# Weights' loads behind the preceding product, and the projection's loads a step later, in a two-block image kernel

## The chip, the cores and the metric

The kernel runs on one core of a Trainium2 chip. A core has a matrix engine (TensorE, PE in the profile; its weight loads are shown as PEld), a vector engine (VectorE, DVE), an activation engine (ScalarE, ACT), a general engine (GpSimd, POOL) and an engine that mostly issues transfers (SyncE, SP). The engines run side by side, each works through its own list of instructions in order, and they wait for each other through semaphores. Transfers between the chip's large memory and the on-chip memory are issued from SP, ACT and POOL.

The metric is the time of one launch on the device in microseconds (us), the median of several runs. Everything is float32.

## The reference, cut to what matters

32 images of 96 x 56 x 56 go through two blocks, and then one normalisation over the whole batch.

```python
# block 0, per image: expand, depthwise 3x3, gate by channel, project, add
h = silu(bn1(conv1x1(x, w1)))            # 96 -> 576 channels
h = silu(bn2(depthwise3x3(h, w2)))
s = sigmoid(W2 @ silu(W1 @ mean_hw(h)))  # one number a channel
x = x + bn3(conv1x1(h * s, w3))          # 576 -> 96: "the projection"

# block 1, per image
mag  = abs(rfft2(x));  ca = gate by channel from mag
sa   = gate by pixel from mean, norm and spectrum of x
y    = x * ca * sa
freq = resize(mean_c(abs(rfft2(y))))
aux  = concat([y, coord, freq])
off  = conv3x3(aux)                      # 9 taps x (dx, dy) a pixel
gate = sigmoid(conv1x1(relu(conv3x3(aux))))
base = conv3x3(y)
smp  = bilinear samples of y at pixel + tap + off
z    = (1 - gate) * base + gate * (def_w . smp)
# at the end, over all images: out = relu(batchnorm(z) + x)
```

## The kernel before, in words

The main part is one long program, `layers`. It works on three images at a time. For image b the main loop samples and convolves block 1, band by band: 7 bands of 8 rows, and each band in two halves. Beside it run two generators: `second(b + 1)` (the function `attend`), which does the gate, the projection, the two Fourier stages and the attention of the next image, and `first(b + 2)` (`hidden`), which expands and does the depthwise convolution of the image after that. `pump` calls them step by step: a band has 17 slots (7 steps of each half, and three more), and each slot lets each generator go on until it has done its share of its steps. `second` has 61 steps, spread over 108 slots of the image's 119. A `yield` in a generator is the end of a step, so an additional `yield` is an empty step.

**The weights.** Sampling is a matrix product. For each half band, weights of 128 x 1008 are made as the product of two tiles, `wc` and `wr`, on VectorE (`weights`, line 692: `wc = wc * wr`). Each of the two tiles is loaded in two parts of 252 KB from `hd` in the large memory, so that is four loads a half band (`weights_load`, lines 685 and 686), issued by SP. There are 448 such products (32 images x 14). `hd` of a band comes from a chain: the offsets are copied out by VectorE (line 651), POOL writes them to memory as `od` (line 655), SP loads them spread over partitions as `ht` (line 667), ScalarE makes hats of them (lines 670 and 671) and writes `hd` (line 674).

`prepare(upto)` issues loads until `upto` products have theirs, and not beyond the bands whose `hd` is written. With `AHEAD = READY = 1`, half band k = 2n + h calls `prepare(k + 2)` at its start, which issues the loads of product k + 1; product k + 1 itself stands in the same half band, behind the first of the two sampling groups (`ready.extend(weights(...))`). `wc` has 3 buffers and `wr` has 2: the loads of product m wait until the sampling of half band m - 3 has read its `wc` (line 721) and until product m - 2 is done.

**The projection.** An image of block 0's hidden values (`h2d`, in the large memory) is read back in 4 pairs of row groups. Each pair has two loads, `hq0` (4 units, 784 KB) and `hq1` (5 units, 980 KB), by `project_loads` (line 305), each with a single buffer. `project` multiplies `hq0` in one step (8 matrix instructions of line 323), then `hq1` in a later step (8 more of line 323 and 4 of line 329). The results go through ScalarE (line 333), POOL adds the residual (line 466) and stores them to `x1d` (line 467). After the fourth pair the first Fourier stage (`dft_mag`) loads `x1d` back (line 361) and multiplies it (lines 386 and 410); its squares are summed on VectorE (line 414).

**Who sets the order.** A scheduler orders the instructions of PE, DVE, ACT and POOL; the order in which the code writes them is its priority. SP is excepted: `tc.manual_schedule(engines={SP})` keeps its instructions in the order of the code. SP therefore holds everything back that stands behind a load that has to wait.

The lines that the change touches are 450 to 468 of `attend` and 1114 to 1135 of the main loop.

## Time and profile before

| | us |
|---|---|
| median of 3 runs (9661.39 to 9698.82) | 9661.97 |
| the profiled execution, own time | 9648.5 |
| its span, first to last instruction | 9646.7 |
| PE busy | 8472.7 (88%) |
| DVE busy | 7227.2 (75%) |
| ACT busy | 5322.1 (55%) |
| POOL busy | 2532.6 (26%) |
| 16 DMA engines' time, the SP queue (q1) | 37.9% of the span |

The page gives, for each engine, the time in which it worked. "Waits" lists name an instruction by engine, tile and line, what it waited for, the total of such waits, how many there were and the longest. The timeline gives the start, the duration, the engine, the line, the operation and the tiles, and in brackets the engine's idle time just before and what ended it. The profile also records the clock that TensorE was granted: in this execution it is either full or half, 0.923 in the mean.

### The profile page before, as it was taken

The page shows a single profiled execution, that of the slowest core. Times are in us where ns is not written, and L with a number is a line of the kernel's source. Part 1 is how long each engine was busy: PE and PEld are TensorE (multiplying, and loading weights), DVE is VectorE, ACT ScalarE, POOL GpSimd, SP SyncE. Part 2 cuts the span into 40 slices and gives each one's busy share as a digit, 9 for nine tenths or more (in the row PEclk, how much of TensorE's full clock was granted, in tenths as well). Part 3 has the DMA queues.
Part 4 walks back from the last instruction along what each step waited for, and adds up shares of the span by engine and source line. Part 5 has one row for each costly group of instructions (what it writes and reads, how often), then busy time and mean ns, then how long its engine had stood idle before and what let it go on. Part 6 is the DMA issues. An engine that isn't in the chain of part 4 may idle for free. (4 is left out here: it accounts for less than half of the span.)

```text
span 9646.7 us, 129705 instructions
## 1 busy us (share of the span) xinstructions
PE 8472.7 (88%) x48374; PEld 5064.2 (52%) x48374; DVE 7227.2 (75%) x6948; ACT 5322.1 (55%) x10262; POOL 2532.6 (26%) x2642
## 2 busy tenths in 40 slices
PE   6889989998999999999899989999999999999870
PEld 3455555555555555555555555555555555555540
DVE  7688777778777787877777887777878777777323
ACT  2355555565555556555555655555555555565453
POOL 1123223222222322222232322233222323322210
PEclk9899999999999999999999999999999999999985
DMA  2355555555555555555555555555555555554449
GB/s 94 95 143 148 151 152 160 150 149 143 147 155 154 160 154 145 145 149 155 154 160 155 145 142 153 151 158 154 153 139 145 150 157 157 153 152 135 130 154 417
DMA packets 1069473, 1485.98 MB, mean 154 GB/s; under 512 B 590438, under 2 KB 840086, under 8 KB 1056550
## 3 DMA queue, kind: packets, MB, share of 16 engines
q1 hardware_dynamic: 858747, 985.20, 37.9%
q10 hardware_dynamic: 153803, 329.80, 9.2%
q0 software_dynamic: 56288, 162.60, 6.7%
q8 instruction: 388, 6.36, 0.3%
q14 instruction: 247, 2.02, 0.1%
HBM read 1064.29 MB, written 412.65 MB: 153 GB/s over the span
## 5 line engine op out<-in xcount | busy, mean ns | idle before, releaser
L261 DVE SCALAR_TENSOR_TENSOR acch<-hp,w,acch 128x1512 f32<-128x1512 f32 (+1 forms) x2250 | 4320.5, 1920 | 32.8
L605 PE MATMUL mm<-yp,c_jointW 104*128 104x448 f32 x4032 | 1649.0, 561 | 9.0 <-ACT yt L709 5.5
L740 PE MATMUL pd<-v,c_def 128*96 128x224 f32 (+1 forms) x6272 | 1414.8, 376 | 127.6 <-ACT v L732 104.1
L703 POOL COPY ybl<-yp 96x448 f32<-96x448 f32 x896 | 1014.7, 1159 | 1903.7 <-PE mm L707 1903.3
L721 PE MATMUL mm<-wc,yt 64*96 64x144 f32 x12544 | 1168.1, 308 | 153.5 <-DVE yb L638 76.8
L740 PEld LDWEIGHTS pd<-v,c_def 128*96 128x96 f32 (+1 forms) x6272 | 1051.8, 173 | 437.4 <-ACT v L732 142.5
L168 PE MATMUL mm<-xt,w 96*128 96x392 f32 (+3 forms) x2688 | 1136.3, 561 | 133.8 <-ACT yt L709 96.0
L605 PEld LDWEIGHTS mm<-yp,c_jointW 104*128 104x128 f32 x4032 | 783.6, 196 | 806.0 <-issue 762.6
L721 PEld LDWEIGHTS mm<-wc,yt 64*96 64x96 f32 x12544 | 884.2, 167 | 489.8 <-issue 188.0
L221 ACT ACTIVATE acch<-acch,sh,inv 128x1568 f32<-128x1568 f32 x288 | 487.5, 1693 | 1159.0 <-DVE acch L261 1143.9
L692 DVE TENSOR_TENSOR wc<-wc,wr 128x1008 f32<-128x1008 f32 x448 | 564.6, 1260 | 704.2 <-DMA wr<-hd 690.5
L725 ACT COPY v<-mm 96x288 f32<-96x288 f32 (+1 forms) x2688 | 1003.6, 442 | 117.7 <-PE mm L721 78.9
L172 ACT ACTIVATE hp<-mm,sh,inv 128x392 f32<-128x392 f32 (+2 forms) x1216 | 811.8, 672 | 326.9 <-PE mm L168 282.1
L633 PE MATMUL mm<-yp,c_base0W 96*64 96x448 f32 x4032 | 913.5, 550 | 0.0
L323 PE MATMUL mm<-hq,w3s 128*96 128x392 f32 x2048 | 788.2, 531 | 127.4 <-DMA hq<-h2d 125.9
L655 POOL DMA_DIRECT2D od<-at x224 | 186.3, 832 | 2275.1 <-DVE at L651 1451.9
L732 ACT COPY v<-v 32x448 f32<-32x448 f32 x1344 | 755.3, 562 | 30.3
L168 PEld LDWEIGHTS mm<-xt,w 96*128 96x128 f32 (+1 forms) x2688 | 389.9, 189 | 495.1 <-issue 264.8
L709 ACT COPY yt<-mm 128x384 f32<-128x384 f32 (+1 forms) x896 | 350.9, 441 | 491.5 <-PE mm L707 489.4
L323 PEld LDWEIGHTS mm<-hq,w3s 128*96 128x96 f32 x2048 | 336.3, 173 | 477.7 <-issue 382.5
L466 POOL TENSOR_TENSOR o<-o,xc 96x392 f32<-96x392 f32 x256 | 396.5, 1549 | 643.9 <-ACT o L333 642.3
L633 PEld LDWEIGHTS mm<-yp,c_base0W 96*64 96x64 f32 x4032 | 294.6, 134 | 515.5 <-issue 490.2
(194 smaller groups left out, 9023.7 us busy)
## 6 DMA issues: line engine op xcount, KB each, us to landing
h2d<-acch ACTq DMA_DIRECT2D x288, 784.0 KB
wc<-hd SPq DMA_DIRECT2D x896, 252.0 KB
wr<-hd SPq DMA_DIRECT2D x896, 252.0 KB
hq<-h2d SPq DMA_DIRECT2D x128, 980.0 KB
hq<-h2d SPq DMA_DIRECT2D x128, 784.0 KB
x<-x1d SPq DMA_DIRECT2D x768, 98.0 KB
ht<-od SPq DMA_DIRECT2D x224, 252.0 KB
hd<-ht ACTq DMA_DIRECT2D x224, 252.0 KB
```

Source lines behind the costliest of these rows:

```text
L168: nc.tensor.matmul(pt[p0 : p0 + w1.shape[1], : rows * W], w1, xts[hf][:, r0 * W : (r0 + rows) * W], start=True, stop=True)
L172: nc.scalar.activation(h1[lo:hi, row0 : row0 + rows, 1 : 1 + W], pt[lo:hi, : rows * W].rearrange("p (h w) -> p h w", h=rows), AF.Silu, bia ...
L261: nc.vector.scalar_tensor_tensor(acc[:, lo:hi], win, wk, acc[:, lo:hi], ALU.mult, ALU.add)
L323: nc.tensor.matmul(pts[half][:C, :EW], w3s[:, ch], hq, start=(i == 0), stop=False)
L605: nc.tensor.matmul(view, weights[:, k], yp[:channels, r0 : r0 + RB, dx + PD - 1 : dx + PD - 1 + W], start=(k == 0), stop=(k == NTAP - 1))
L633: nc.tensor.matmul(pb[k % 2 * BC : (k % 2 + 1) * BC, :BW].rearrange("p (h w) -> p h w", h=RB), w["base"][:, k], yp[:C, r0 : r0 + RB, dx + ...
L692: nc.vector.tensor_tensor(wc, wc, wr, ALU.mult)
L703: nc.gpsimd.tensor_copy(yb[:, :, s], blocks)
L721: nc.tensor.matmul(pt[k][:C, (t - lo) * KP : (t - lo + 1) * KP], yt[ps, t], s[ps, t * KP : (t + 1) * KP], start=True, stop=True)
L725: nc.scalar.copy(v[:C, :, lo:hi, k].rearrange("c k t p -> c t k p"), pt[k][:C, : (hi - lo) * KP].rearrange("c (t k p) -> c t k p", t=hi - ...
L732: nc.scalar.copy(v[C:, 1 + 2 * i : 3 + 2 * i], v[i * QC : (i + 1) * QC, KA:])
L740: nc.tensor.matmul(out.rearrange("c q (t x) -> c t q x", x=TS), p["w"]["def"][ks, k], v[ks, k].rearrange("c t s (r x) -> c t (s r) x", r=T ...
```

## The change

```diff
 def attend(...):                       # the projection, pair q of 4
         for q in range(NQ):
+            if q:
+                yield
             at = q, q + NQ
             xrs = [residual_load(nc, p, x, k) for k in at]
             outs = project(nc, p, rows)
             next(outs)
             yield
+            yield
             if q + 1 < NQ:
                 first = project_loads(nc, p, h2d, q + 1, 0)
-            yield
             os = next(outs)
-            if q + 1 < NQ:
-                rows = [first, project_loads(nc, p, h2d, q + 1, 1)]
             yield
             for k, o, xr in zip(at, os, xrs):
                 nc.gpsimd.tensor_tensor(o, o, xr, ALU.add)
                 nc.gpsimd.dma_start(x1[:, k * EW : (k + 1) * EW], o)
+            if q + 1 < NQ:
+                rows = [first, project_loads(nc, p, h2d, q + 1, 1)]
             yield

 # the main loop, band n, half h
                 v = p["vp"].tile([128, NTAP, NTH, 2, TP], FP, name="v")
-                prepare(2 * n + h + READY + AHEAD)
                 s = ready.pop(0)
                 ...
                         ready.extend(weights(nc, *ws) for ws in loads[:1])
                         del loads[:1]
+                        prepare(2 * n + h + 1 + READY + AHEAD)
                         if h == 0:
                             yts.append(block_channels(nc, p, yp, j, 1))
```

Half band k now issues the loads of product k + 2, directly behind product k + 1, where before the loads of product k + 1 stood at the start of half band k. So each group of four loads stands four slots earlier in the code or, across a band's end, seven. In the projection, `hq0` of the next pair is issued two steps behind the product that frees its buffer (one step before), and `hq1` one step behind its own (in the same step before). Pairs 1 to 3 have 5 steps instead of 4, so `second` has 64 steps instead of 61 in the same 108 slots. No instruction and no byte is added or taken away in the image loop, except what the scheduler places itself.

## The prediction

> **What bounds the kernel now.** I read the page first, then the list of waits on PE and on DVE, then the timeline around the two waits that the change aims at.

> ```profile
> span 9646.7 us, 129705 instructions
> PE 8472.7 (88%) x48374; PEld 5064.2 (52%) x48374; DVE 7227.2 (75%) x6948; ACT 5322.1 (55%) x10262; POOL 2532.6 (26%) x2642
> ```

> PE bounds it. From the first product of weights (445 us) to the last (9348 us) one image takes 278.2 us, and PE is idle in it for 753.0 us in all, 23.5 an image. In the same stretch the clock record shows half speed for 1110.9 us; work done at half speed takes twice as long, so up to 555 us more lie there.

> ```profile
> PE mm L323 <- DMA hq<-h2d: 125.9, 31, 9.4
> PE pd L740 <- ACT v L732: 104.1, 84, 5.4
> PE mm L168 <- ACT yt L709: 96.0, 44, 5.2
> PE mm L707 <- ACT sq L413: 80.3, 21, 6.5
> PE mm L721 <- DVE yb L638: 76.8, 55, 6.1
> PE acc L430 <- DVE m_fe L427: 43.1, 31, 4.2
> ...
> DVE wc L692 <- DMA wr<-hd: 690.5, 152, 18.3
> ```

> PE's greatest single wait is on the projection's loads, once an image. PE hardly ever waits for a product of weights itself; VectorE does, for 690 us, and it works in order.

> Cut by product (number 0 to 13 in an image, 32 images averaged; DVE idle just before the product / PE idle from it to the next / half clock in that stretch): 0: 3.0 / 4.3 / 4.7; 1: 0.4 / 2.7 / 5.4; 2: 3.2 / 2.1 / 1.7; 5: 5.7 / 6.3 / 10.7; 7: 0.3 / 2.9 / 3.3; 9: 0.3 / 2.5 / 4.1; 10: 0.6 / 1.9 / 2.1; 12: 5.9 / 0.2 / 0.2; all others under 1 of each, bar 1.4 half clock at 6. So product 12's wait costs PE nothing, product 5's goes with the worst stretch, and stretch 0 is the `hq` wait. The timeline of one image:

> ```profile
> 4145.10 2.88 PE L323 MATMUL mm<-hq,w3s 128*96 128x392 f32 x8
> 4148.00 9.08 SPq L305 DMA_DIRECT2D hq<-h2d  x2
> 4161.09 4.37 PE L323 MATMUL mm<-hq,w3s 128*96 128x392 f32 x8 [3.59 <-DMA hq<-h2d]
> ...
> 4225.69 0.67 SPq L667 DMA_DIRECT2D ht<-od  x1
> 4228.15 0.58 SPq L685 DMA_DIRECT2D wc<-hd  x1
> 4230.08 0.58 SPq L686 DMA_DIRECT2D wr<-hd  x1
> ...
> 4240.81 1.21 DVE L692 TENSOR_TENSOR wc<-wc,wr 128x1008 f32<-128x1008 f32 x1 [4.86 <-DMA wr<-hd]
> 4242.67 1.00 ACT L413 ACTIVATE sq<-mm 128x464 f32<-128x464 f32 x2 [4.73 <-DVE s L414]
> 4243.28 0.47 PE L707 MATMUL mm<-c_ident,ybl 96*128 96x96 f32 x3 [1.12 <-ACT sq L413]
> 4248.26 0.93 PE L168 MATMUL mm<-xt,w 96*128 96x392 f32 x2 [2.03 <-ACT yt L709]
> 4251.09 0.55 PE L430 MATMUL acc<-c_RT,m_fe 128*29 128x112 f32 x2 [1.90 <-DVE m_fe L427]
> ```

> First part: the last `hq0` is issued when its buffer comes free (4148.0), lands 13.1 us later, and PE has only some 11 us of other work; behind the wait the same eight matmuls take 4.37 us instead of 2.88. Second part: product 5 holds VectorE for 4.86 us; the sum behind it (L414) is late, ScalarE's square waits 4.73 us, and PE then waits three times.

> **The change part by part.** The sum is against the profiled execution's 9648.5 us; the median, 9662.0, is 13.5 above it.

> *(a) hq.* I take the order that the scheduler gives PE in the changed program, and PE's busy time per instruction of this profile's rows. Before, from the end of one `hq0` product to the start of the next PE has 14.1, 18.4 and 11.1 us of work; after the change 24.5, 13.5 and 24.5. For `hq1` it is 22.8, 13.4, 13.2 before (where nothing waited) and 23.7, 13.4, 22.8 after. The tight 11.1 is gone; the least is 13.5 (12.2 in every second image) against a landing of 13.1 that had `hq1` and five weight and hat loads (1.26 MB) ahead of it. In the changed list only one weights group stands between the pairs. So the 126 us go. Of the half clock, 89 us begin right behind these waits; half is lost, 44 us. I take -170; bounds 0 (the wait returns at the 12.2) and -170.

> [...]

> *(b) The weights' loads.* Relative to a product, its first load is issued 11.6 to 23.3 us before (medians by number), its last 9.2 to 20.8. The buffers are free and `hd` is issued well before that: sampling m - 3 ends 23 to 51 us before product m, except for number 7 (17.3) and number 5 (13.4). In the changed list, groups 12, 13, 0 and 1 stand ahead of a pair of `hq` loads that they stood behind, and group 2 ahead of the first loads of `x1d`, for which SP waited until 4187.3. So the DVE waits at 12, 0 and 2 go: 12.1 us an image, 388 us of VectorE. PE gains little, since stretch 12 has no idle and stretch 0 is already in (a): I take -20, bounds 0 and -90 (all of stretch 2's idle, 66, and half its half clock, 27).

> Group 5 is different. It stood behind `ht` and still does; `ht` waits for `od`, and the sampling of 2 ends 13.4 us before the product anyway. Its loads cannot be issued much earlier. But VectorE reaches the product later: between the copies of line 651 and product 5 it now has some 19 us of work by these rows, against 13.4. The landing is 18.7 us behind the copies (4222.1 to 4240.8), so the wait falls from 5.7 to about 1. Against that, products 4 and 5 now stand ahead of all three sums of L414 (before, the first sum was ahead of 5). And L430 stands behind 8 of line 605's matmuls (over 3 us of work) instead of behind one expansion. Stretch 5 costs 6.3 idle + 5.3 clock = 11.6 us an image, 371 in all. I take 3.5 us an image, -110; bounds +50 (the sums later by product 5's 1.2 us, 38, and its clock) and -371.

> *(c) Three more steps.* The projection ends later: 23 of 64 steps instead of 20 of 61, some 3 slots, 7 us. What follows it is denser. In the scheduler's order PE has 10.8 or 12.1 us of work between the last L329 and the first L386, against 19.5 or 20.7 before. That cover hid the chain through ScalarE, POOL's two adds, the store to `x1d` and its loads. Images 0 and 1, with no cover, show it: 13.4 and 10.7 us from the end of L329 to L386, with SP's loads at +8.3 and +7.6. In the others SP issues at about +9.5, so L386 could start at +12.6 to +14.6. That leaves 0.5 to 3.8 us an image uncovered. I take 2.2 us, 70, and 30 for clock: +100; bounds 0 and +300 (POOL's adds late as well).

> *(d) The rest.* The second Fourier stage gets two of its three L410 groups back to back; the nearest row is L410's own wait, 1.0 us in all: +10, bounds 0 and +60 (if its bank waits like L707's in stretch 5). Issued earlier, the weights can hold SP: group 7 now stands ahead of the second stage's six `x1d` loads and waits for the sampling of 4 (17.3 us before product 7 at 4290.2), so these go at about 4275 instead of 4268.7; POOL multiplies them from 4292.3 on, so nothing; without that cover 6.7 us x 32 = 214. Group 6 holds the load of the next-but-one image until `hd` (4254.4); that is used an image later, nothing. Four more table loads on ScalarE at 1.28 us: nothing, it is idle 45%. The prologue's empty steps: nothing, the expansion of image 1 runs in them; at most 3 x 5 us.

> Sum: -170 - 20 - 110 + 100 + 10 = -190. Not all of that stays. PE reaches the stretches 1, 7 and 9 earlier, and their waits (L709, L725, L638, m_fy) end by ScalarE and VectorE, which the change does not shorten. I keep two thirds, -130, an estimate. 9648.5 - 130 + 13.5 = 9532.

> [...]

> **Rivals.**
> *Slower: the chain to `x1d` takes over.* For: cover down by 8.7 us, POOL works in order with stores of z and od between the adds (POOL waited 756.8 us for z in all). Against: in images 2 to 30 the add ended by +5.7 to +7.9. In POOL's changed list the last two adds stand behind a store of z where they stood behind one of od. Price: every uncovered us is 32, and half as much in clock, 48. Without (c) the sum is -290, so it decides from 6 us, an L386 that can start only 17.5 us behind L329; at 7 us it is +46, 9708, at 8 us 9756.
> *The gain is given back.* A wait on ScalarE or VectorE takes each one's place: stretches 1, 7, 9 and 10 hold 10.0 us of idle an image already, none of it from loads. Against: VectorE loses 388 us of waiting itself. 9662, give or take 45.
> *Stretch 5 goes wholly.* If the sums come in time: -371 instead of -110, so -450 in sum, two thirds: 9362. For: VectorE's later arrival. Against: both products ahead of the sums.
> *The loads are not earlier,* since SP is held by something else (it waits 1273 us for L386). That is (b) at nothing and (a) kept, within the forecast's own range.

> **How the numbers follow.** The forecast, 0.45, with its own range 9440 to 9610; stretch 5 wholly, 0.15; given back, 0.17; slower, 0.23. Bounds together: 9350 to 9760 leaves out about 0.1 on either side. A measurement tells about 0.5% (48 us) from no change. Faster: 0.45 + 0.15 + a little of the third, 0.61; within: 0.14; slower: 0.23 + 0.02.

> **What would show it.** Right: L323 <- hq under 20 us; L692 <- wr under 350 us, with what is left at product 5; SP's wait of L305 on L329 and L323 (1352 us) much shorter. (c): a new wait of L386 on x, around 70 us. Wrong: L323 <- hq as before; L707 <- sq over 80; L386 <- x over 250; or PE's idle unchanged under other names.

## The result, and the profile after

The changed kernel takes 9817.2 us (median of 4 runs, 9768.17 to 9840.77) against 9676.99 us of the kernel before on the same chip (9661.39 to 9698.82). The ratio is 1.0137, with a 95% interval from 1.0088 to 1.0185: slower, where faster was forecast, and outside the stated range. The profiled execution, 9768.17 us, is the fastest of the four, so the profile below accounts for 120 us of the 140.

The page of the changed kernel begins so (in it all lines from 470 on have numbers higher by 2):

```profile
span 9766.4 us, 129877 instructions
PE 8643.2 (88%) x48374; PEld 5161.4 (53%) x48374; DVE 7240.5 (74%) x6948; ACT 5335.4 (55%) x10266; POOL 2735.1 (28%) x2642
```

PE's instructions are the same 48374, and its idle time fell, from 1174.0 us (9646.7 - 8472.7) to 1123.2. What rose is its busy time, by 170.5 us: the same work, most of it at a lower clock. The mean granted clock went from 0.923 to 0.911, and between the first and last products of weights half speed is recorded for 1374.1 us instead of 1110.9. In this trace neighbouring matmuls of line 742 start 189 ns apart at full clock and 373 at half, those of line 323 329 and 653 (medians), so half of the 263 us is taken as lost: 132 us. Some 40 us of the longer busy time are thus not in the clock.

The list of PE's waits in the changed kernel (total, number, longest):

```profile
PE mm L723 <- DVE yb L640: 175.6, 91, 4.8
PE acc L430 <- DVE m_fe L427: 151.8, 30, 7.2
PE mm L386 <- DMA x<-x1d: 74.1, 20, 5.5
...
PE mm L323 <- DMA hq<-h2d: 12.9, 3, 7.8
```

The wait on `hq` is gone (125.9 before), those on `sq` and `yt` nearly (80.3 and 96.0). In their place stand `yb` (76.8 before), `m_fe` (43.1 before), both made by VectorE, and the expected new wait on `x` (17.9 before).

The waits of VectorE and of SP that answer to the prediction's part (b), in the changed kernel:

```profile
DVE wc L694 <- DMA wr<-hd: 736.4, 205, 20.2
DVE sq L372 <- DMA x<-x1d: 278.3, 32, 11.2
```

```profile
SPq L687 <- DMA hd<-ht: 1819.0, 191, 35.0
...
SPq L305 <- PE mm L329: 790.6, 96, 9.0
SPq L305 <- PE mm L323: 615.8, 95, 11.6
```

VectorE waits for the loads of the weights longer than before (736 against 690), though every load is written earlier. And SP now stands at those loads because `hd` is not yet there: 1819 us, where the kernel before had this line:

```profile
SPq L685 <- DMA hd<-ht: 702.6, 42, 24.3
```

How both come together shows in the timeline of image 15 of the changed kernel, at product 12:

```profile
4725.43 0.80 ACT L672 ACTIVATE ht<-ht,c_blk 112x576 f32<-112x576 f32 x1
4727.64 0.33 ACTq L676 DMA_DIRECT2D hd<-ht  x1
...
4730.32 0.60 SPq L687 DMA_DIRECT2D wc<-hd  x1
...
4732.26 0.64 SPq L688 DMA_DIRECT2D wr<-hd  x1
...
4742.75 1.21 DVE L694 TENSOR_TENSOR wc<-wc,wr 128x1008 f32<-128x1008 f32 x1 [4.97 <-DMA wr<-hd]
...
4743.99 0.69 DVE L653 COPY at<-mm 18x224 f32<-18x224 f32 x2
4744.71 0.63 ACT L630 ACTIVATE yb<-mm,c_cvec 32x448 f32<-32x448 f32 x1 [4.32 <-DVE at L653]
...
4745.39 0.48 PE L723 MATMUL mm<-wc,yt 64*96 64x144 f32 x2 [1.28 <-ACT yb L630]
```

The hats are stored at 4727.64, SP issues the loads 2.7 us later, the last of them at 4732.26, and the product can start 10.5 us after that. VectorE has stood at it for 4.97 us. The copies of the next band's offsets (L653) come behind it, ScalarE's `yb` behind those, and PE's sampling behind `yb`. The sampling that needs product 12 itself is far off: in the changed kernel a product starts 27.7 us in the mean before its sampling, against 16.5 before. An even product (the first of a band) starts 17.5 us after its `hd` was stored (median), against 31.9.

### The profile page after: what moved, and what is told of

It is laid out like the page before. It is cut to its first block, busy times and chain, and to the rows that moved or that the text cites. A ratio compares the mean times of both kernels' runs of the same rounds, so it can differ in the third digit from the quotient of the medians.

```text
span 9766.4 us, 129877 instructions
## 1 busy us (share of the span) xinstructions
PE 8643.2 (88%) x48374; PEld 5161.4 (53%) x48374; DVE 7240.5 (74%) x6948; ACT 5335.4 (55%) x10266; POOL 2735.1 (28%) x2642
## 3 DMA queue, kind: packets, MB, share of 16 engines
q14 instruction: 248, 2.03, 0.1%
## 5 line engine op out<-in xcount | busy, mean ns | idle before, releaser
L705 POOL COPY ybl<-yp 96x448 f32<-96x448 f32 x896 | 1278.4, 1453 | 2032.6 <-PE mm L709 2024.7
L742 PE MATMUL pd<-v,c_def 128*96 128x224 f32 (+1 forms) x6272 | 1455.2, 383 | 70.6 <-ACT v L734 43.9
L723 PE MATMUL mm<-wc,yt 64*96 64x144 f32 x12544 | 1220.5, 319 | 251.8 <-DVE yb L640 175.6
L742 PEld LDWEIGHTS pd<-v,c_def 128*96 128x96 f32 (+1 forms) x6272 | 1079.0, 178 | 393.9 <-issue 90.0
L723 PEld LDWEIGHTS mm<-wc,yt 64*96 64x96 f32 x12544 | 928.0, 175 | 618.9 <-issue 210.5
L168 PE MATMUL mm<-xt,w 96*128 96x392 f32 (+3 forms) x2688 | 1153.5, 562 | 53.1 <-DMA xt<-in_x 33.3
L607 PEld LDWEIGHTS mm<-yp,c_jointW 104*128 104x128 f32 x4032 | 758.2, 191 | 749.2 <-issue 703.9
L635 PE MATMUL mm<-yp,c_base0W 96*64 96x448 f32 x4032 | 946.7, 572 | 0.0
L323 PE MATMUL mm<-hq,w3s 128*96 128x392 f32 x2048 | 744.1, 507 | 14.8 <-DMA hq<-h2d 12.9
L386 PE MATMUL mm<-c_FU,x 112*128 112x116 f32 x3072 | 497.9, 314 | 132.8 <-DMA x<-x1d 74.1
L386 PEld LDWEIGHTS mm<-c_FU,x 112*128 112x128 f32 x3072 | 446.3, 220 | 271.0 <-issue 91.0
L168 PEld LDWEIGHTS mm<-xt,w 96*128 96x128 f32 (+1 forms) x2688 | 377.4, 189 | 369.1 <-issue 231.8
```

What stands on the lines that cost most here:

```text
L168: nc.tensor.matmul(pt[p0 : p0 + w1.shape[1], : rows * W], w1, xts[hf][:, r0 * W : (r0 + rows) * W], start=True, stop=True)
L323: nc.tensor.matmul(pts[half][:C, :EW], w3s[:, ch], hq, start=(i == 0), stop=False)
L386: nc.tensor.matmul(pt[:, i * 4 * V : (i + 1) * 4 * V], x2s[g][:, 2 * i : 2 * i + 2, :].rearrange("h c w -> h (c w)"), w["FU"], start=True, ...
L607: nc.tensor.matmul(view, weights[:, k], yp[:channels, r0 : r0 + RB, dx + PD - 1 : dx + PD - 1 + W], start=(k == 0), stop=(k == NTAP - 1))
L635: nc.tensor.matmul(pb[k % 2 * BC : (k % 2 + 1) * BC, :BW].rearrange("p (h w) -> p h w", h=RB), w["base"][:, k], yp[:C, r0 : r0 + RB, dx + ...
L705: nc.gpsimd.tensor_copy(yb[:, :, s], blocks)
```

## The experiments

Ratios are against the kernel before on the same chip. Two theories stood at the start: the weights' part costs, because their products are placed earlier than `hd` allows (A), or the empty steps of the projection cost (B).

**The two parts alone.** `e1` is the kernel before with the main loop's part only, `e2` the kernel before with the projection's part only.

```diff
-                prepare(2 * n + h + READY + AHEAD)               # e1
...
+                        prepare(2 * n + h + 1 + READY + AHEAD)
```

```diff
+            if q:                                                # e2, and the loads a step later
+                yield
...
+            yield
             if q + 1 < NQ:
                 first = project_loads(nc, p, h2d, q + 1, 0)
-            yield
```

> The loads behind the preceding product, with the projection as before. Two theories. A, the weights are the cause: with their loads further ahead in the code the scheduler puts each product some 14 us earlier on VectorE (median lead over its sampling 14.0 us before, 29 after), while the chain od, ht, hat, hd is not earlier, so VectorE still waits at the products (over 650 us in all), SP waits for hd over 1500 us, and half clock stays near 1370 us; and the hq wait of 126 us is back: slower than before by 150 to 250 us. B, the three empty steps are the cause, since they move the Fourier stages against the bands: then this one is within 50 us of before or faster, and the waits of L430 on m_fe (152 us after) and of L721 on yb L638 (176 us after) are near the 43 and 77 of before.

> The projection as changed, the weights' loads as before. A (weights are the cause): faster than before by 80 to 170 us, the hq wait under 20 us, VectorE's wait at the products near the 690 us of before, SP's wait for hd near 700 us. B (the empty steps are the cause): slower than before by about 140 us, with the wait of L430 on m_fe near 150 us and half clock over 1300 us.

Measured: weights alone 9809.97 us, 1.0172 [1.0131, 1.0214]; projection alone 9914.22, 1.0258 [1.0219, 1.0298]. Each part alone makes the kernel slower, and by more than both together, so the loss is not one part's alone. `e1` is what theory A said, with SP waiting 1567.0 us on `hd` and VectorE 736.6 at the product, bar one thing: PE's wait on `hq` did not come back (9.9 us). `e2` is slower than either theory said, though B's signs came (L430 waits 155.3 us on `m_fe`, and 43.7 us an image are at half clock). In it something else happens. Its timeline, image 15, just ahead of the projection:

```profile
4521.85 1.21 DVE L694 TENSOR_TENSOR wc<-wc,wr 128x1008 f32<-128x1008 f32 x1 [12.11 <-DMA wr<-hd]
4523.09 0.17 DVE L292 TENSOR_TENSOR s<-acc,seb 128x5 f32<-128x5 f32 x1
4523.29 0.21 ACT L293 ACTIVATE s<-s 128x5 f32<-128x5 f32 x1 [9.80 <-DVE s L292]
...
4523.74 0.66 DVE L296 TENSOR_TENSOR w3s<-w,s 128x480 f32<-128x480 f32 x1
...
4524.50 2.24 PE L323 MATMUL mm<-hq,w3s 128*96 128x392 f32 x3 [7.41 <-ACT v L734]
```

The list of waits names ScalarE's copy of `v` for PE's 7.41 us, but PE starts when VectorE has written the scaled weights of the projection, `w3s`. VectorE could not, because it stood for 12.11 us at a product; that product's loads were issued late, behind `hq1`, for which SP had waited 14.2 us. So in `e2`, too, PE waits for a product that it does not yet need. Moving the weights ahead takes this one away (band 0 loses 13.3 us an image to idle and clock in `e2`, 6.3 in the changed kernel), which is some 220 us of the 280 by which the parts do not add.

**The product written later.** `e3`: the changed kernel, the product two steps into the second sampling group. `e4`: the changed kernel with the first group of each band loaded at the half band's start again.

```diff
-                        ready.extend(weights(nc, *ws) for ws in loads[:1])
+                        due_now = loads[:1]          # e3: multiplied when i == 1, second step
```

```diff
+                if h == 1:                           # e4, at the start of the half band
+                    prepare(2 * n + h + READY + AHEAD)
...
-                        prepare(2 * n + h + 1 + READY + AHEAD)
+                        if h == 1:
+                            prepare(2 * n + h + 1 + READY + AHEAD)
```

> The changed kernel, with each product of weights written two steps into the second sampling group instead of ahead of it, its loads left where the change put them. A: the product moves later on VectorE, so its wait falls well below 736 us, to 300 or less, the half clock of 10 us an image behind product 12 goes, and the time comes to 9550 to 9700. If the products' place does not matter (B): near 9817, with yb and m_fe waits as in the changed kernel.

> The changed kernel, with the even groups (the first of each band, which follow hd) back at the start of the half band and only the odd ones early. A: SP's wait for hd falls from 1819 us to near 700, even products go back to a lead of 14 us over their sampling, half clock falls below 1200 us, and the time is below the changed kernel's by 80 to 200 us. B: no change against 9817 beyond 40 us.

Measured: `e3` 9763.19, 1.0105 [1.0075, 1.0135]; `e4` 10301.23, 1.0671 [1.064, 1.0703]. In `e3` the product still starts 27.3 us before its sampling, and VectorE waits 705.7 us: writing it later did not make it later, because the scheduler, not the place in the code, sets VectorE's order. So `e3` does not test what a later product would do. `e4` brought a new wait (PE's L284 on `acch`, 266.4 us, against 14.0) and answers nothing; its cause was not followed.

**The product pinned.** `e5`: the changed kernel with the product kept behind what the code puts before it on VectorE. `e6`: the same in the kernel before.

```diff
-    nc.vector.tensor_tensor(wc, wc, wr, ALU.mult)
+    p["tc"].keep_in_program_order(nc.vector.tensor_tensor(wc, wc, wr, ALU.mult))
```

> The changed kernel with the product of weights kept on VectorE behind everything that the code puts there before it, so that it can no longer be placed by when its loads land. Theory P (the early place of the product on VectorE is what costs): its wait on wr falls from 736 us to under 450, the place in band 0 where the clock halves 16 to 17 us after the joint convolution starts (266 us at half clock) goes or shrinks to a third, and the time is 9640 to 9740, near the kernel before. Theory D (any rearrangement that makes PE's short waits stand closer together keeps the clock low, and this kernel's product is not the reason): VectorE's wait may fall, but the half clock stays at 39 us an image or more, and the time is 9770 to 9880.

> The kernel before with the same pin, as the control of the run above: in it the product already stands some 15 us ahead of its sampling, and VectorE waits 690 us. Theory P: the pin takes waits from VectorE here too, under 450 us, and the time is 9560 to 9680. Theory D: the order around the product changes as it does in any rearrangement, the half clock rises from 34.8 us an image to 39 or more, and the time is 9720 to 9850.

Measured: `e5` 9531.3, 0.9867 [0.9841, 0.9893]; `e6` 9452.7, 0.9805 [0.9781, 0.9828]. One line takes 2.7% from the changed kernel and 2.0% from the one before. VectorE's waits in `e5`:

```profile
DVE sq L372 <- DMA x<-x1d: 277.9, 33, 10.0
...
DVE wc L694 <- DMA wr<-hd: 194.6, 52, 10.4
```

and in `e6`:

```profile
DVE wc L692 <- DMA wr<-hd: 403.3, 93, 20.3
```

Both times are lower than theory P gave, and D's half clock of 39 us an image did not come (35.6 and 29.0); only the half clock in band 0 shrank less than P said, from 9.37 to 5.43 us an image. VectorE's 736 became 195, and 690 became 403. The product's lead fell from 27.7 to 19.6 us and from 16.5 to 12.2. So the scheduler had placed the product too early on VectorE. SP still waits 1683.9 us on `hd` in `e5`: in the changed kernel SP's own wait is not what costs most, VectorE's is.

**The hat values taken away.** `e7`: the changed kernel, weights from the `hd` of the band before, so that no load has to wait for its own band.

```diff
-                loads.append(weights_load(nc, p, hds[n], m))
+                loads.append(weights_load(nc, p, hds[max(0, n - 1)], m))
```

> The changed kernel with the weights loaded from the hat values of the band before (the output is therefore not the reference's; nothing else is left out), so that no load and no product has to wait for the hat values of its own band. SP's wait of wc on hd (1819 us) falls to under 300 in either theory. Theory P, that the wait of product 12 for hat values is what halves the clock in band 0: VectorE's wait in front of product 12 (5.8 us an image) falls under 2, the 266 us of half clock there go, and the time falls by 100 to 200, to 9620 to 9720. Theory D: the half clock moves to another place, 39 us an image or more, and the time stays above 9750.

Measured: 9538.12, 0.9886 [0.9862, 0.9909], 2.5% under the changed kernel, with the product as early as there (28.5 us before its sampling). VectorE's and SP's lists:

```profile
DVE wc L694 <- DMA wr<-hd: 561.3, 191, 19.0
```

```profile
SPq L361 <- PE mm L386: 905.7, 163, 47.8
SPq L687 <- PE mm L723: 898.9, 136, 16.7
```

SP now stands at the weights for another reason, the buffer (899 us), and the time is lower all the same. VectorE's idle time at product 12 fell from 5.9 to 3.4 us an image (under 2 was expected), at product 10 from 4.0 to 0.1, and the half clock in band 0 from 9.37 to 2.80 us an image. The time is below P's range. What else this edit moves in the scheduler's order was not separated.

**The empty steps.** `e8`: the changed kernel without the empty step ahead of the pairs.

```diff
-            if q:
-                yield
```

> The changed kernel without the empty step ahead of each pair of the projection but the first (three an image); the shifts of the hq loads and the weights stay. Theory E (the empty steps push the projection's end against the first Fourier stage and cost 74 us of PE's waits of L386 on x, and clock): that wait falls under 30 us, PE's wait on hq rises to 20 to 130, and the time is 9680 to 9760. Theory D: the half clock stays at 39 us an image or more and the time above 9770.

Measured: 9836.59, 1.0211 [1.0177, 1.0244]. PE's wait on `hq` is back (115.7 us, 33 times) and that of L386 did not go (174.0 on POOL, 50.1 on `x`). So with the other edits in place the empty steps keep the `hq` wait away, and they are not what makes the change slow, as theory D said. They are not needed for it: `e1` has none, and waits 9.9 us (see (a) below). One wait does come and go with them: L430 on `m_fe` is 46.4 us here, 47.7 in `e1`, 62.8 and 62.6 in `e6` and `e9` below and 43.1 before, but 108 to 155 in all the kernels with the empty steps that are told of here (`e2` to `e5`, `e7`, `e10`, `e12`, `e13`).

**Both parts, pinned.** `e9` and `e10` are `e1` and `e2` with the pin, `e11` is `e6` with the product written as late as in `e3`.

> The weights' part alone, with the product kept on VectorE where the code puts it. Theory P (VectorE's wait in front of the product is what the part costs): the wait falls from 737 us to 200 to 450 and the time from 9810 to 9430 to 9540, no slower than the pinned kernel before (9453) by more than 1%. Theory R (the earlier loads cost something of their own, for instance SP held by the wait on hd): SP's wait on hd stays over 1500 us and the time is 9580 or more, beyond the pinned changed kernel (9531).

> The projection's part alone, pinned in the same way. In it the product led its sampling as in the kernel before (16.9 us), but VectorE's wait was 840 us and the time 9914. Theory P: the wait falls under 500 us and the time to 9500 to 9650. Theory R (the projection's part costs by itself: the last steps of the projection stand close to the first Fourier stage and the first product of a pair waits): the time stays over 9700, and over the pinned kernel before by more than 2.6%.

> The kernel before, pinned, with the product written two steps into the second sampling group, so that it stands later still. Theory P, that waits of VectorE are what is left to take: its wait falls from 403 us to under 250 and the time from 9453 to 9370 to 9440. Rival: the sampling behind it is reached too soon, PE waits for the product (a wait of the sampling on wc of 50 us or more, now absent), and the time is 9480 to 9600.

Measured: `e9` 9615.15, 0.9965 [0.995, 0.998]; `e10` 9843.74, 1.0202 [1.0181, 1.0223]; `e11` 9587.56, 0.9939 [0.9922, 0.9956]. `e9` gains 2.0% by the pin, but is 1.6% slower than `e6`, so theory R has it: SP waits 1592.3 us on `hd`, though VectorE waits only 178.4 at the product. Its PE waits 291.1 us at L386 (`e6`: 158.6). So without the projection's part the earlier loads cost something besides VectorE's wait; what it is was not separated. `e10` gains 0.5%, as R said: its product is in front of `w3s` in the code as well, and the pin keeps it there (VectorE still idles 11.4 us an image at product 12, and PE's first L323 waits 244 us in all). `e11` shows the other end. VectorE's wait falls to 118.7, but PE now waits 121.3 us, 54 times, at the sampling; 50 of those samplings, for products 7 and 9, start 0.1 us behind the end of their product. So the product can be too late as well.

**What is left of the change.** `e12` is `e5` with the hat values of the band before; `e13` and `e14` cut the steps between the hats' load and first use in the two pinned kernels; `e15` and `e16` are the kernel before and its pinned form with the hat values of the band before.

```diff
-    for _ in range(6):                    # e13, e14: in offsets(), behind the load of ht
+    for _ in range(3):
         yield
```

> The pinned changed kernel with the weights loaded from the hat values of the band before (the output is therefore not the reference's; nothing else is left out). Theory S (what the pinned changed kernel still loses, 78 us, is SP held at the weights' loads): SP's wait on hd falls from 1684 to under 300 us, and the time from 9531 to 9400 to 9470. Theory T (it is the three steps more and what they do to the clock): the wait on hd goes all the same, and the time stays at 9500 to 9560.

> The pinned changed kernel with the wait between the hat values' load and their first use cut from six steps to three, so that the hat values are stored some 6 us earlier; nothing else is changed. Theory S: SP's wait on hd falls by a third or more (from 1684 to under 1150 us) and the time from 9531 to 9430 to 9510. Theory T: the wait on hd falls and the time stays at 9500 to 9570; ScalarE, in order, may now wait for ht (a new wait of the Abs on ht), which would add to the time.

> The pinned kernel before with the same shorter wait for the hat values. Its SP waits on hd only 513 us, so theory S gives it less than e13: 9420 to 9460, VectorE's wait of 403 us under 350. Theory T: within 0.5% of 9453, or slower where ScalarE waits for ht.

> The kernel before with the weights loaded from the hat values of the band before (the output is therefore not the reference's; nothing else is left out). SP waits on hd only 703 us in the kernel before, against 1819 in the changed one, where the same edit gave 279 us. Theory G (the change is a gain once hat values are early): 9580 to 9650, slower than the changed kernel with the same edit (9538). Theory T (the change costs by itself as well): under 9530.

> The pinned kernel before with the hat values of the band before (the output is not the reference's; nothing else is left out), against 9445 us of the changed kernel with both edits. Theory G: 9450 to 9500, so the change's own remainder is nothing or a small gain. Theory T: 9350 to 9420, so that the change costs 30 to 90 us by itself.

Measured: `e13` 9528.43, 0.9875 [0.9847, 0.9903], the same as `e5`, though SP's wait on `hd` fell from 1684 to 1199; `e14` 9481.02, 0.9814 [0.9795, 0.9833], the same as `e6`. `e15` (9628.51 us) and `e16` (9453.61) lie in theory G's ranges, and with `e12` they close a table of ratios:

| | before | changed | changed / before, 95% from both intervals |
|---|---|---|---|
| as it is | 1 | 1.0137 | 1.014 ± 0.005 |
| hat values of the band before | 0.9969 (`e15`) | 0.9886 (`e7`) | 0.992 ± 0.003 |
| pinned | 0.9805 (`e6`) | 0.9867 (`e5`) | 1.006 ± 0.004 |
| both | 0.9797 (`e16`) | 0.9778 (`e12`) | 0.998 ± 0.003 |

Early hat values give the kernel before 0.3%, the changed one 2.5%. With them the change is a gain of 0.8%, as theory G had it; with the pin as well there is no difference. So what makes the change a loss is, for the most part, the lateness of the hat values against products placed early: taking away the lateness turns the loss into a gain, and taking away the early place, by the pin, leaves 0.6 of its 1.4%. Pinned, the changed kernel gains another 0.9% by early hat values (`e12`, 9445.06, 0.9778 [0.9761, 0.9796], inside theory S's range). How it does that stays open: `e13`, with hat values 31.2 instead of 26.6 us ahead of an even product and SP's wait 29% shorter, gained nothing, against S.

## Why the prediction was wrong, step by step

Time lost an image (PE's idle time and half of the half-clock time), cut at the joint convolutions of the bands, 29 images; idle time is counted in the band of the instruction that waited:

| bands | before | changed | `e7` | `e5` | `e6` |
|---|---|---|---|---|---|
| 0 to 2 (projection, first Fourier) | 15.4 | 13.9 | 11.1 | 11.9 | 14.8 |
| 3 and 4 (product 5, L414, L430) | 13.1 | 11.7 | 12.1 | 9.3 | 4.1 |
| 5 and 6 | 11.8 | 17.4 | 13.5 | 16.2 | 14.9 |
| an image's length | 281.9 | 286.0 | 280.2 | 280.4 | 275.4 |

Over 32 images the change gives -49, -44 and +182 us, and another +43 us is in neither idle time nor the clock. The -49 hides two large terms: band 0, where product 12 stands, goes from 0.1 to 6.3 us an image (about +200), and bands 1 and 2, the projection's own, give about 250 back.

*(a), the wait on `hq`: right in size, but not for the reason in the change.* 125.9 became 12.9, and the half clock of band 1 went with it (4.59 to 0.00 us an image). SP's waits of L305 on L323 and L329, a sign named for being right, did not get shorter (1352 us before, 1406 now). In the kernel before, the changed one, `e1`, `e2`, `e8` and `e9` alike, SP issues `hq0` of pairs 1 to 3 at the moment when its buffer comes free (0.03 us behind the product before it, median), so writing it a step later in the code moved nothing. What counts here is what SP has issued just ahead of the last `hq0`, and how much time PE leaves it. In one image of `e1` (the first view) the weights stand behind it, in one of `e8` (the second) ahead of it:

```profile
4236.78 0.36 SPq L305 DMA_DIRECT2D hq<-h2d  x1
4237.19 0.60 SPq L685 DMA_DIRECT2D wc<-hd  x1
...
4246.12 2.80 PE L323 MATMUL mm<-hq,w3s 128*96 128x392 f32 x8
```

```profile
4229.24 0.57 SPq L686 DMA_DIRECT2D wr<-hd  x1
...
4232.12 9.08 SPq L305 DMA_DIRECT2D hq<-h2d  x2
...
4244.40 4.42 PE L323 MATMUL mm<-hq,w3s 128*96 128x392 f32 x8 [2.77 <-DMA hq<-h2d]
```

In `e1` it has landed within 9.3 us; with the four weights loads (1.0 MB) ahead of it, it takes 12.3 us in `e8` and, with a hat load besides, 13.1 before. So the weights' part alone takes the wait away (`e1` 9.9 us, `e9` 11.4). In the changed kernel the group stands ahead again, but the empty steps leave 21.9 us (median) instead of the 13.2 of before, its wait included. In these rows `hq0` thus takes 2.9 us or more longer with a group ahead; the 21.9 us are more than any of the three landings, and the wait did not come back (12.9 us in all).

*(b), the weights' loads: the step that failed.* -20 was taken for it. It said "`hd` is issued well before that", and from it "So the DVE waits at 12, 0 and 2 go: 12.1 us an image". Measured at 12, 0 and 2 in the changed kernel: 5.9, 3.6 and 0.1 us; 690 us in all became 736. The step took the product to stay where it was while its loads moved. In fact the scheduler put the product 11 us earlier along with the loads, so it starts 13.3 us (median) behind its first load, as before (15.2). And the chain that makes `hd` was not earlier: the 31.9 us between its storing and an even product, which the step called well before, shrank to 17.5, of which the landing of the hats, the four issues and the landing of the weights take 15.1 in the timeline above. That was all the room there was, and the change used it up. The waits at 12 and 0 stayed, and a new one came at product 10: VectorE's idle there went from 0.5 to 4.0 us, and SP's hold in front of that group from 0.5 to 12.7. "Stretch 12 has no idle" did not hold any longer either: from product 12 to 13 PE now idles 1.5 us an image and runs 9.0 us at half clock.

*Product 5's stretch: wrong, and it shows the same.* -110 was taken, -44 came in bands 3 and 4. The wait at product 5 went only from 5.8 to 3.4 us, not to about 1. L430 was to be covered by line 605's matmuls; it waits 151.8 us instead of 43.1. The rival "Stretch 5 goes wholly" had the right mechanism and the wrong edit: it is what the pin alone does in the kernel before. In `e6` VectorE does not wait at product 5, and bands 3 and 4 lose 4.1 us instead of 13.1, 288 us over 32 images, of which 99 come back in bands 5 and 6 (11.8 to 14.9).

*(c), the three steps: right.* L386 waits 74.1 us on `x`, +56 over before, where 70 was taken. VectorE's new wait at L372 on `x` (30.2 to 278.3 us) was not foreseen; it stays in `e5` (277.9) and `e7` (275.0), which are quicker than the kernel before, so it does not by itself make the change a loss. What it costs was not measured.

*The rivals and the sum.* "The gain is given back" named the right lines (`yb`, waits that end by VectorE), but argued that VectorE had 388 us less waiting. It had not. Bands 5 and 6, where product 10 stands, took +182 us, and band 0 with product 12 about +200; the rest gave less than that. The slower rival, the chain to `x1d`, did not happen.

*The clock.* It was priced only beside the waits that were to go or come (44 us in (a), 30 in (c)). The sign of the result lies there for the greater part: PE's idle time fell by 51 us, the clock took 132 us, and the time rose.

## What to carry to other kernels

A load is early only from the moment when its source is written: before moving one, measure the room between the last write of its source and its use, and not only the buffers and the queue (here 31.9 us, of which the change left 17.5). Where a scheduler orders an engine, moving a load can move its consumer too, as it did here by 11 us, and the engine can then stand at something that nobody needs yet, with urgent work behind it, as VectorE did for 4.97 us at product 12 of image 15; look at what is queued behind the waiting instruction, and pin the consumer to its place. Here that one pin, without the change, gives 9452.7 us, 2.0% under the kernel before.

## What the hardware showed that was not expected

In this trace half clock follows short waits of PE and lasts longer than they do. The stretches of the changed kernel around the place of image 15 shown above, from the view by stretches (start and end, length; busy us and number of instructions of PE, PEld, DVE, ACT and POOL; granted clock of TensorE; share of the DMA engines' time; GB/s):

```profile
4740.00:4747.00 7.00, 5.32 (x31) 2.41 (x25) 2.87 (x5) 2.65 (x5) 1.90 (x3) 1.00 0.66 217
4747.20:4757.40 10.20, 10.09 (x39) 6.73 (x40) 1.83 (x5) 6.23 (x15) 0.00 (x0) 0.50 0.65 193
4757.50:4764.00 6.50, 6.50 (x44) 4.92 (x43) 5.79 (x5) 1.49 (x5) 1.27 (x2) 1.00 0.58 174
```
